# A recurrence's transposes moved from TensorE to VectorE and DMA, in three of seven groups

## The chip, the core and the metric

The kernel runs on one core of a Trainium2 chip. A core has TensorE (matrix products and transposes, called PE in the profile; its weight loads are shown apart as PEld), VectorE (DVE), ScalarE (ACT), GpSimd (POOL), and SyncE (SP), which here only issues DMAs. Each engine works through its own queue in order, and semaphores tie the queues together. The metric is the device time of one execution in microseconds.

## The reference

The input is x, 3327 tokens of 256 features in fp32, and a sparse adjacency matrix. Two layers follow. Layer 0 is graph attention with two heads, and then a mixture of 16 experts, of which each token takes two. Layer 1 is graph attention with one head, and then a recurrence. The change lies in the recurrence, which runs 30 steps on a state h of 3327 x 256:

```python
def step(h, _):
    h = h + 0.01 * jnp.tanh(h)
    h = h * jax.nn.sigmoid(h)
    h = _layernorm(h, ln_w, ln_b)
    h = jnp.einsum('bsc,dc->bsd', h, W) + b
    return (h, None)
```

The result of the recurrence is added to x. Tokens don't mix in the recurrence: a step is a chain for each token, and different tokens are independent.

## The kernel before, in words

Tokens lie on the 128 partitions: 26 tiles of 128 tokens, with the 256 features along the free dimension. The tile x in SBUF holds the state of all tokens; it stays on chip for all 30 steps. The recurrence (L865 to L902) loops over steps, and in a step over seven groups of tiles: six of four tiles, numbers 0 to 5, and number 6 of two.

For one group of a step:

- ScalarE takes the tanh (L871), GpSimd adds it to the state (L873), ScalarE applies silu (L874). The state is kept scaled by S = 100, so the factor 0.01 needs no instruction. The result is z.
- VectorE takes the statistics of z for each tile (bn_stats, L879, and bn_aggr, L859), and GpSimd makes 1/sqrt(var + eps) of them (L861, L862), called rr.
- The layer norm's mean, weight and bias are folded into the matrix beforehand: wc is the weighted matrix with its column mean taken out, and bb is the bias row (L833 to L846). So z can be multiplied without being normalized first, and rr is applied to the product.
- A product contracts over the features, and the operand that TensorE keeps as weights has to have them on the partitions. So TensorE transposes z, two blocks of 128 x 128 per tile, into the PSUM tile pt (L881), and ScalarE copies pt to SBUF as zT (L883).
- TensorE multiplies (L887): for each tile, two products with zT as weights and wc as the moving operand, added up in the PSUM tile po. [...]the trace has four matmul records a tile, 104 a step.
- VectorE writes the new state, x = po * rr + bb (L892).

In the last step the kept input is added (L899) and the output leaves by DMA.

Every tile of a group comes from a pool with a fixed number of buffers: th, z and zT have two each (pool "steps"), and so have the PSUM tiles pt and po[...]. A tile's next use waits until the readers of the buffer's earlier use are done.

The code is written in a straight line for one group after another. The framework that builds the program turns it into the engines' queues: it puts instructions that are ready by its own estimate in order of the program, and adds the semaphore waits. Thus the order on a queue is fixed before the run, and it is not the order of the source: in the trace, TensorE transposes two groups and then multiplies two groups. The names and lines above are those that the change touches; attend (L186, called at L829 for layer 1) is the attention that runs before.

Of the kernel before, what the change touches and what calls it, by code (L numbers as in the profile page):

```python
# [10 lines left out]
F32 = mybir.dt.float32  # L11
# [8 lines left out]
P = 128  # L20
# [3 lines left out]
S = 100.0  # L24
G = 4
MOST = 6


@with_exitstack
def gat_moe_gat_recurrent_ffn(ctx: ExitStack, tc: tile.TileContext, a: dict, out: bass.AP):  # L30
    nc = tc.nc
    N, D = a["x"].shape
    KD = D // P
# [9 lines left out]
    groups = [range(t, min(t + G, NT)) for t in range(0, NT, G)]  # L43
# [265 lines left out]
    lb = rec.tile([P, KD], F32, name="lb")  # L309
    fb = rec.tile([P, D], F32, name="fb")  # L310
    wc = rec.tile([P, KD, D], F32, name="wc")
    bb = rec.tile([P, D], F32, name="bb")
    ones_r = rec.tile([P, P], F32, name="ones_r")
    wv1 = rec.tile([P, KD, D + 2], F32, name="wv1")
# [453 lines left out]
    with ExitStack() as st:  # L768
        keep = st.enter_context(tc.tile_pool(name="keep2", bufs=1))
        wh = keep.tile([P, NT, 1, D + 1], F32, name="wh")  # L770
        sc = Scores(keep, 1)
        nc.vector.memset(wh[:, :, :, D : D + 1], 1.0)
        work = st.enter_context(tc.tile_pool(name="work2", bufs=2))
        ps = st.enter_context(tc.tile_pool(name="ps2", bufs=2, space=PSUM))
        ps_o = st.enter_context(tc.tile_pool(name="ps2o", bufs=2, space=PSUM))
        def add_results(some):
            for ts in some:
                n, two = len(ts), []
                for k, name in enumerate(("th", "z")):
                    here = slice(k * NP + ts[0] * P, k * NP + (ts[-1] + 1) * P)  # L780
                    two.append(steps.tile([P, G, D], F32, name=name)[:, :n, :])
                    nc.sync.dma_start(two[k], given[here, :].rearrange("(t p) d -> p t d", p=P))
                (nc.vector if ts is groups1[0] else nc.gpsimd).tensor_tensor(two[0], two[0], two[1], ALU.add)  # L783
                here = x[:, ts[0] : ts[-1] + 1, :]
                nc.vector.tensor_tensor(here, here, two[0], ALU.add)

        add_results(groups1[:2])
        count = 0

        def spot():  # L790
            nonlocal count
            count += 1
            return ps_o.tile([P, 512], F32, name=f"acc{count % 3}")

        def split1(t, p):
            nc.scalar.copy(wh[:, t, 0, :D], p[:, :D])
            nc.vector.tensor_copy(sc.s[:, t, :, 0], p[:, D : D + 2])
            for ts in groups1:
                if t == ts[-1]:
                    sc.finish(ts[0], t + 1)  # L800

        project(
            groups1, wv1, D + 2, split1, work, ps, spot, True,
            lambda ts, power: add_results(groups1[groups1.index(ts) + 2 :][:1]),
        )
        nc.vector.tensor_scalar(wh[:, NT - 1], wh[:, NT - 1], real[:, 0:1], None, op0=ALU.mult)

        run = st.enter_context(tc.tile_pool(name="edge2", bufs=3))
        rows_p = st.enter_context(tc.tile_pool(name="rows2", bufs=2))
        fin = st.enter_context(tc.tile_pool(name="fin2", bufs=2))  # L810

        def add_elu(t, pr, h, po, r):

            low = fin.tile([P, D], F32, name="low")
            high = fin.tile([P, D], F32, name="high")
            nc.vector.tensor_scalar(low[:pr], po, r, 0.0, op0=ALU.mult, op1=ALU.min)
            nc.vector.tensor_scalar(high[:pr], po, r, 0.0, op0=ALU.mult, op1=ALU.max)  # L817
            nc.scalar.activation(low[:pr], low[:pr], AF.Exp)
            nc.vector.scalar_tensor_tensor(high[:pr], low[:pr], -1.0, high[:pr], op0=ALU.add, op1=ALU.add)
            nc.vector.tensor_tensor(x[:pr, t, :], x[:pr, t, :], high[:pr], ALU.add)  # L820

        def begin_state(ts):
            here = slice(ts[0] * P, (ts[-1] + 1) * P)
            nc.sync.dma_start(kept[here, :].rearrange("(t p) d -> p t d", p=P), x[:, ts[0] : ts[-1] + 1, :])
            yield
            tiles = [x[:, t, :] for t in ts]
            normalized(tiles, tiles, S)

        attend(sc, wh, 1, groups2, 1, add_elu, begin_state, (run, rows_p, ps, ps_o), deque())  # L829

        pb = ps.tile([P, 512], F32, name="bank")[:, :D]  # L833
        for k in range(KD):
            nc.tensor.matmul(
                pb, lhsT=lb[:, k : k + 1].to_broadcast([P, P]), rhs=fW[:, k, :], start=(k == 0), stop=(k == KD - 1)
            )
        nc.vector.tensor_tensor(bb, pb, fb, ALU.add)
        nc.vector.tensor_scalar(bb, bb, S, None, op0=ALU.mult)
        pc = ps.tile([P, 512], F32, name="bank")[:, :D]  # L840
        for k in range(KD):
            nc.vector.tensor_scalar(wc[:, k, :], fW[:, k, :], lw[:, k : k + 1], None, op0=ALU.mult)
            nc.tensor.matmul(pc, lhsT=ones_r, rhs=wc[:, k, :], start=(k == 0), stop=(k == KD - 1))
        for k in range(KD):
            nc.vector.scalar_tensor_tensor(wc[:, k, :], pc, -1.0 / D, wc[:, k, :], op0=ALU.mult, op1=ALU.add)
            nc.vector.tensor_scalar(wc[:, k, :], wc[:, k, :], S, None, op0=ALU.mult)  # L846


    with ExitStack() as st:
        ps_t = st.enter_context(tc.tile_pool(name="ps3t", bufs=2, space=PSUM))  # L850
        ps_o = st.enter_context(tc.tile_pool(name="ps3o", bufs=2, space=PSUM))
        last_p = st.enter_context(tc.tile_pool(name="last", bufs=2))

        def inv_norm(stats, n):


            v = small.tile([P, G, 2], F32, name="v")
            for j in range(n):
                nc.vector.bn_aggr(v[:, j, :], stats[:, j, :])  # L859
            r = small.tile([P, G], F32, name="rr")  # L860
            nc.gpsimd.tensor_scalar(r[:, :n], v[:, :n, 1], EPS, None, op0=ALU.add)  # L861
            nc.gpsimd.tensor_tensor(r[:, :n], r[:, :n], neg_half[:, :n], ALU.pow)  # L862
            return r

        for step in range(N_STEPS):  # L865
            for ts in groups:
                n = len(ts)
                hs = x[:, ts[0] : ts[0] + n, :]
                th = steps.tile([P, G, D], F32, name="th")
                z = steps.tile([P, G, D], F32, name="z")  # L870
                nc.scalar.activation(th[:, :n, :], hs, AF.Tanh, scale=1.0 / S)  # L871

                nc.gpsimd.tensor_tensor(th[:, :n, :], th[:, :n, :], hs, ALU.add)  # L873
                nc.scalar.activation(z[:, :n, :], th[:, :n, :], AF.Silu, scale=1.0 / S)  # L874
                stats = small.tile([P, G, 6], F32, name="stats")
                pt = ps_t.tile([P, G, KD, P], F32, name="pt")
                zT = steps.tile([P, G, KD, P], F32, name="zT")
                for j in range(n):
                    nc.vector.bn_stats(stats[:, j, :], z[:, j, :])  # L879
                    for k in range(KD):  # L880
                        nc.tensor.transpose(pt[:, j, k, :], z[:, j, k * P : (k + 1) * P], ident)  # L881
                rr = inv_norm(stats, n)
                nc.scalar.copy(zT[:, :n, :, :], pt[:, :n, :, :])  # L883
                po = ps_o.tile([P, G, D], F32, name="po")
                for j in range(n):
                    for k in range(KD):
                        nc.tensor.matmul(  # L887
                            po[:, j, :], lhsT=zT[:, j, k, :], rhs=wc[:, k, :],
                            start=(k == 0), stop=(k == KD - 1),
                        )  # L890
                for j in range(n):
                    nc.vector.scalar_tensor_tensor(  # L892
                        x[:, ts[0] + j, :], po[:, j, :], rr[:, j : j + 1], bb, op0=ALU.mult, op1=ALU.add
                    )
                if step == N_STEPS - 1:
                    here = slice(ts[0] * P, (ts[-1] + 1) * P)
                    old = last_p.tile([P, G, D], F32, name="old")
                    nc.sync.dma_start(old[:, :n, :], kept[here, :].rearrange("(t p) d -> p t d", p=P))
                    nc.vector.scalar_tensor_tensor(  # L899
                        hs, hs, 1.0 / S, old[:, :n, :], op0=ALU.mult, op1=ALU.add  # L900
                    )
                    move_pairs(out, hs, ts[0] // 2, (ts[-1] + 1) // 2, True)  # L902
# [49 lines left out]
```

## Time and profile before

The kernel took 2091.18 us, the median of 3 runs (2089.25 to 2093.39). The profiled execution spans 2089.5 us at a mean granted TensorE clock of 0.979 of full speed.

| in the recurrence | per | number |
|---|---|---|
| TensorE products, L887 | 3120 records | 705.5 us busy |
| TensorE transposes, L881 | 1560 records | 189.9 us busy |
| GpSimd add, L873 | 210 instructions | 461.2 us busy |
| GpSimd power, L862 | 210 instructions | 207.5 us busy |
| VectorE state, L892 | 780 instructions | 324.9 us busy |
| VectorE statistics, L879 | 780 instructions | 283.8 us busy |
| ScalarE copy, L883 | 210 instructions | 199.1 us busy |
| ScalarE silu, L874, and tanh, L871 | 210 instructions each | 210.6 and 199.3 us busy |

How to read it: busy times of different engines lie beside each other, and do not add up. What sets the time is the engine that has no idle time, or a chain of instructions that wait for each other. A line of a timeline gives the start, the duration, engine, line, operation, the tile written and those read, and in square brackets how long the engine sat idle before and for whom. Names on the left of an arrow are written, those on the right are read. SPq is SP's queue of DMA issues; the duration there is that of the issue, not of the transfer.

### The profile page before, as it was taken

To read this page: it belongs to the slowest core of one execution; us is meant where nothing else is said; L and a number is where in the kernel's file an instruction comes from. 1 tells how busy PE (TensorE), PEld (TensorE's weight loads), DVE (VectorE), ACT (ScalarE), POOL (GpSimd) and SP (SyncE) were. 2 spreads that over 40 slices of the span, in tenths; PEclk is the share of its full clock that TensorE was granted. 3 is DMA by queue.
4 is the path that set the end of the run, shared out by engine and by line. 5 is a ranking of instruction groups with operands and counts; after the bars stand their busy time and mean duration, and the time that the engine had idled before them with its cause. 6 is when DMAs were issued, how large, how long until landed. Compare 5 with 4: busy or idle time off the path is not lost.

```text
span 2089.5 us, 34134 instructions
## 1 busy us (share of the span) xinstructions
PE 1974.8 (95%) x12252; PEld 1788.9 (86%) x12252; DVE 1304.8 (62%) x3824; ACT 1110.9 (53%) x1455; POOL 965.7 (46%) x896
## 2 busy tenths in 40 slices
PE   7999999749999997899999999999999999999998
PEld 6899999749999997688888888888888888888887
DVE  6787887712222222557766777777777777777777
ACT  2876766501111111656655666666566656665664
POOL 2010211343333332401100187777777777777775
PEclk9999999869999999899999999999999999999999
DMA  7878050067888883200000100000000000000003
GB/s 151 110 104 115 2 81 16 26 183 244 275 299 280 277 268 117 82 8 8 16 8 16 34 1 1 1 1 1 1 1 1 1 1 1 1 1 1 1 1 111
DMA packets 133438, 148.79 MB, mean 71 GB/s; under 512 B 51886, under 2 KB 95735, under 8 KB 133269
## 3 DMA queue, kind: packets, MB, share of 16 engines
q1 hardware_dynamic: 116577, 112.19, 17.9%
q0 software_dynamic: 12016, 29.66, 8.2%
q10 hardware_dynamic: 4676, 4.76, 0.8%
q8 instruction: 98, 1.61, 0.3%
q14 instruction: 71, 0.58, 0.1%
HBM read 174.37 MB, written 30.56 MB: 98 GB/s over the span
## 4 chain that ended last, share of the span: by engine, by line
PE 71%; ACT 5%; issue 1%; POOL 1%; DVE 1%; DMA 1%; SPq 0%; POOLq 0%; ACTq 0%; DVEq 0%
PE po L887 34%; PE acc L246 14%; PE pa L720 6%; PE pb L720 6%; PE po L751 6%; PE pt L881 4%; ACT zT L883 4%; PE pt L711 1%; PE acc L153 1%; POOL lists L551 0%; DMA z<-given 0%; PE bank L139 0%; POOL th L783 0%; DMA rows<-table_x,which 0%; POOL rstd L119 0%
## 5 line engine op out<-in xcount | busy, mean ns | idle before, releaser
L887 PE MATMUL po<-wc,zT 128*128 128x256 f32 x3120 | 705.5, 383 | 21.9 <-ACT zT L883 21.3
L887 PEld LDWEIGHTS po<-wc,zT 128*128 128x128 f32 x3120 | 582.9, 190 | 124.9 <-ACT zT L883 50.5
L246 PE MATMUL acc<-wh,pT 128*128 128x129 f32 (+1 forms) x4056 | 607.2, 311 | 7.0 <-DVE pT L241 6.7
L246 PEld LDWEIGHTS acc<-wh,pT 128*128 128x128 f32 x4056 | 563.7, 192 | 44.7 <-DVE pT L241 8.3
L236 ACT ACTIVATE e<-rb,minus,full 128x384 f32<-128x384 f32 (+3 forms) x494 | 401.3, 824 | 180.1 <-DVE pT L241 163.7
L873 POOL TENSOR_TENSOR th<-th,x 128x1024 f32<-128x1024 f32 (+1 forms) x210 | 461.2, 2214 | 63.7 <-ACT th L871 63.7
L241 DVE SCALAR_TENSOR_TENSOR pT<-e,part,adjT 128x384 f32<-128x384 f32 (+3 forms) x494 | 380.3, 773 | 146.3 <-PE acc L246 122.2
L892 DVE SCALAR_TENSOR_TENSOR x<-po,rr,bb 128x256 f32<-128x256 f32 x780 | 324.9, 477 | 118.2 <-PE po L887 113.4
L883 ACT COPY zT<-pt 128x1024 f32<-128x1024 f32 (+1 forms) x210 | 199.1, 948 | 332.7 <-PE pt L881 332.7
L879 DVE BATCH_NORM_STATS2 stats<-z 128x6 f32<-128x256 f32 x780 | 283.8, 415 | 117.5 <-ACT z L874 117.5
L119 POOL TENSOR_TENSOR rstd<-ve,neg_half 128x4 f32<-128x4 f32 (+3 forms) x28 | 31.2, 1116 | 408.0 <-DVE ve L117 312.4
L862 POOL TENSOR_TENSOR rr<-rr,neg_half 128x4 f32<-128x4 f32 (+1 forms) x210 | 207.5, 988 | 17.4
L874 ACT ACTIVATE z<-th 128x1024 f32<-128x1024 f32 (+1 forms) x210 | 210.6, 1003 | 0.9 <-POOL th L873 0.9
L871 ACT ACTIVATE th<-x 128x1024 f32<-128x1024 f32 (+1 forms) x210 | 199.3, 995 | 2.3 <-DVE x L128 1.4
L881 PE MATMUL pt<-ident,z 128*128 128x128 f32 x1560 | 189.9, 273 | 2.5 <-DVE high L817 2.5
L881 PEld LDWEIGHTS pt<-ident,z 128*128 128x128 f32 x1560 | 177.8, 141 | 14.8 <-issue 2.9
L744 DVE TENSOR_TENSOR hidT<-act,pb 128x512 f32<-128x512 f32 x67 | 46.1, 688 | 219.7 <-PE pb L720 216.2
L741 ACT ACTIVATE act<-pa 128x512 f32<-128x512 f32 x67 | 40.0, 597 | 205.1 <-PE pa L720 202.0
L720 PEld LDWEIGHTS pa<-hT,ew 128*128 128x128 f32 x1072 | 131.5, 194 | 5.0 <-ACT hT L712 1.7
L685 POOL DMA_INDIRECT rows<-table_x,which x67 | 64.6, 964 | 152.4 <-PE pt L711 136.8
L551 POOL DMA_INDIRECT lists<-pair,ati x52 | 60.2, 1157 | 160.8 <-DVE ati L538 85.2
L720 PE MATMUL pa<-hT,ew 128*128 128x128 f32 x1072 | 132.1, 277 | 1.0 <-ACT hT L712 1.0
(173 smaller groups left out, 1392.3 us busy)
## 6 DMA issues: line engine op xcount, KB each, us to landing
ew<-in_w_dram SPq DMA_DIRECT2D x201, 512.0 KB
in_bytes<-in_adj_dram POOLq DMA_DIRECT2D x3, 2496.0 KB, 28.2
x<-in_x_dram SPq DMA_DIRECT2D x6, 512.0 KB
th<-given SPq DMA_DIRECT2D x6, 512.0 KB
z<-given SPq DMA_DIRECT2D x6, 512.0 KB
kept<-x SPq DMA_DIRECT2D x8, 384.0 KB
old<-kept SPq DMA_DIRECT2D x6, 512.0 KB
out_dram<-x SPq DMA_DIRECT2D x6, 512.0 KB
```

Source lines behind the costliest of these rows:

```text
L236: nc.scalar.activation(e[:, : n * P], rb[:, : n * P], AF.Relu, scale=sc.full[:, j, h : h + 1], bias=sc.minus[:, j, h : h + 1],)
L241: masked = nc.vector.scalar_tensor_tensor(pT[:, : n * P], e[:, : n * P], sc.part[:, j, h : h + 1], adjT[:, j // 2, ts[0] * P : (ts[-1] + 1 ...
L246: nc.tensor.matmul(po[c], lhsT=pT[:, c * P : (c + 1) * P], rhs=wh[:, j, h, :], start=(j == 0 and c % per_bank == 0), stop=(j == NT - 1), s ...
L720: nc.tensor.matmul(p[:, f, :], lhsT=w[:, k, f * P : (f + 1) * P], rhs=hT[:, k, :], start=(k == 0), stop=(k == KD - 1),)
L862: nc.gpsimd.tensor_tensor(r[:, :n], r[:, :n], neg_half[:, :n], ALU.pow)
L873: nc.gpsimd.tensor_tensor(th[:, :n, :], th[:, :n, :], hs, ALU.add)
L874: nc.scalar.activation(z[:, :n, :], th[:, :n, :], AF.Silu, scale=1.0 / S)
L879: nc.vector.bn_stats(stats[:, j, :], z[:, j, :])
L881: nc.tensor.transpose(pt[:, j, k, :], z[:, j, k * P : (k + 1) * P], ident)
L883: nc.scalar.copy(zT[:, :n, :, :], pt[:, :n, :, :])
L887: nc.tensor.matmul(po[:, j, :], lhsT=zT[:, j, k, :], rhs=wc[:, k, :], start=(k == 0), stop=(k == KD - 1),)
L892: nc.vector.scalar_tensor_tensor(x[:, ts[0] + j, :], po[:, j, :], rr[:, j : j + 1], bb, op0=ALU.mult, op1=ALU.add)
```

## The change

Groups 0, 2 and 4 of every step no longer have z transposed by TensorE. VectorE transposes the blocks of 32 x 32 in one instruction over the whole group (128 x 1024), writing a tile tz in which the four tiles of the group are innermost. A block transpose turns each block, but leaves it in its own quarter of the partitions. So sixteen DMAs, from SBUF to SBUF, then move the quarters: quarter a of the partitions and feature blocks 2b and 2b + 1 of tz go to quarter b of a tile zx. Each moves 32 partitions times 1024 bytes, 32 KB, in runs of 512 bytes. All are issued by SP. The products read their weights from zx with a stride of four elements, 16 bytes. As the features now lie on the partitions in another order, the moving operand is wx, a copy of wc with its rows in that order, made once by eight small DMAs. The tiles tz and zx have two buffers each. For these groups the tiles pt and zT and ScalarE's copy fall away. Groups 1, 3, 5 and 6 stay as they were.

The purpose is to take work off TensorE. The call of the attention of layer 1 was moved behind the making of wc, bb and wx in the source, so that these come earlier in the program.

```diff
+QUAD = 32
...
+    wx = rec.tile([P, KD, D], F32, name="wx")
...
-        attend(sc, wh, 1, groups2, 1, add_elu, begin_state, (run, rows_p, ps, ps_o), deque())
-
...
+        for k in range(KD):
+            for q in range(4):
+                first = (2 * k + q // 2) * QUAD
+                nc.sync.dma_start(wx[first : first + QUAD, q % 2, :], wc[q * QUAD : (q + 1) * QUAD, k, :])
+
+        attend(sc, wh, 1, groups2, 1, add_elu, begin_state, (run, rows_p, ps, ps_o), deque())
...
+        swap_p = st.enter_context(tc.tile_pool(name="swap", bufs=2))
+
+        def exchanged(z):
+            tz = swap_p.tile([P, D // QUAD, QUAD, G], F32, name="tz")
+            nc.vector.transpose(
+                tz.rearrange("p b t j -> p j b t"), z.rearrange("p j (b t) -> p j b t", t=QUAD)
+            )
+            zx = swap_p.tile([P, KD, P, G], F32, name="zx")
+            for a in range(P // QUAD):
+                for b in range(P // QUAD):
+                    nc.sync.dma_start(
+                        zx[b * QUAD : (b + 1) * QUAD, :, a * QUAD : (a + 1) * QUAD],
+                        tz[a * QUAD : (a + 1) * QUAD, 2 * b : 2 * b + 2],
+                    )
+            return zx
...
-                pt = ps_t.tile([P, G, KD, P], F32, name="pt")
-                zT = steps.tile([P, G, KD, P], F32, name="zT")
+                swap = ts in groups[0:6:2]
+                if swap:
+                    zx = exchanged(z)
+                else:
+                    pt = ps_t.tile([P, G, KD, P], F32, name="pt")
+                    zT = steps.tile([P, G, KD, P], F32, name="zT")
                 for j in range(n):
                     nc.vector.bn_stats(stats[:, j, :], z[:, j, :])
-                    for k in range(KD):
-                        nc.tensor.transpose(pt[:, j, k, :], z[:, j, k * P : (k + 1) * P], ident)
+                    if not swap:
+                        for k in range(KD):
+                            nc.tensor.transpose(pt[:, j, k, :], z[:, j, k * P : (k + 1) * P], ident)
                 rr = inv_norm(stats, n)
-                nc.scalar.copy(zT[:, :n, :, :], pt[:, :n, :, :])
+                if not swap:
+                    nc.scalar.copy(zT[:, :n, :, :], pt[:, :n, :, :])
...
-                            po[:, j, :], lhsT=zT[:, j, k, :], rhs=wc[:, k, :],
-                            start=(k == 0), stop=(k == KD - 1),
+                            po[:, j, :], lhsT=zx[:, k, :, j] if swap else zT[:, j, k, :],
+                            rhs=(wx if swap else wc)[:, k, :], start=(k == 0), stop=(k == KD - 1),
```

## The prediction, made before the changed kernel was run

> **What bounds the kernel now.** I read the page's 40 slices first, then the busy time in a window of the recurrence, then the chain of work that ended last inside that window, then the timeline of one pair of groups, then the waits.
>
> The slices split the span. The recurrence is the last 17 or so of 40: TensorE at 9 tenths throughout, VectorE and GpSimd at 7, ScalarE at 6, DMA engines at 0.
>
> ```profile
> PE   7999999749999997899999999999999999999998
> DVE  6787887712222222557766777777777777777777
> ACT  2876766501111111656655666666566656665664
> POOL 2010211343333332401100187777777777777775
> DMA  7878050067888883200000100000000000000003
> ```
>
> Eleven steps of it, busy us for each engine:
>
> ```profile
> 1607.00:1937.00 330.00, 322.22 (x1721) 279.95 (x1722) 240.74 (x863) 209.04 (x233) 261.09 (x233) 1.00 0.00 1
> ```
>
> The block of 32 matmuls that starts at 1606.96 starts again at 1636.86, so one step takes 29.90 us, and 30 steps 897 us: they run from 1186 us, the first transpose, to the end. Per step TensorE is busy for 29.2 us (98%), VectorE 21.8, GpSimd 23.7, ScalarE 18.9. The clock is 1.00, so no throttle is to be won back.
>
> The chain in this window, in order of time:
>
> ```profile
> 1606.96 7.17 PE po L887 x32
> 1614.14 0.89 PE pt L881 x8
> 1615.03 0.02 issue
> 1615.05 1.02 ACT zT L883
> 1616.07 0.04 issue
> 1616.11 7.17 PE po L887 x32
> ```
>
> A pair of groups (8 tiles) is one turn of 9.15 us. The products take 7.17, the first group's transposes 0.89, then comes ScalarE's copy of 1.02, under which TensorE makes the second group's transposes. From the timeline of the same turn:
>
> ```profile
> 1606.81 1.06 ACT L874 ACTIVATE z<-th 128x1024 f32<-128x1024 f32 x1
> 1606.96 7.17 PE L887 MATMUL po<-wc,zT 128*128 128x256 f32 x32 [0.23 <-ACT zT L883]
> 1613.97 1.91 PE L881 MATMUL pt<-ident,z 128*128 128x128 f32 x16
> 1616.11 7.17 PE L887 MATMUL po<-wc,zT 128*128 128x256 f32 x32 [0.23 <-ACT zT L883]
> ```
>
> The square brackets give TensorE's only wait: 0.23 us a pair. And z of the next pair is ready at 1607.87, yet its products start at 1616.11: z leads them by **8.2 us**. VectorE's waits are slack, since what it waits for is TensorE or the z that TensorE's pace holds back:
>
> ```profile
> DVE stats L879 <- ACT z L874: 45.2, 78, 1.1
> DVE x L892 <- PE po L887: 42.2, 33, 1.5
> PE po L887 <- ACT zT L883: 7.8, 34, 0.2
> ```
>
> So TensorE sets the end, and its transposes (L881) lie on its path.
>
> [...]Both new strides (VectorE's write of tz, TensorE's weights from zx) are exactly 16 bytes, and nothing in this trace shows that case. [...]a 256 KB load issued at 826.45 released VectorE at 829.61, 3.2 us later, of which its bytes need about 1 at the 250 to 300 GB/s of the page's busy slices.
>
> **Removed.** For groups 0, 2 and 4 the eight transposes each: a half of the 1.91 us for sixteen, or the 0.89 of the chain. Three times 0.89 is **2.7 us a step on the path**, 80 us in 30 steps. Three ScalarE copies of 1.0 us go too, off the path, for ScalarE has 11 us idle a step. Three of seven uses of pt in PSUM go, and no wait in the window is put down to its buffers.
>
> **Added on VectorE.** One transpose of 128x1024 fp32 for each of three groups. [...]I take 1.25, with something for the waits on the buffer's earlier readers. VectorE goes from 21.8 to 25.6 us a step. That is within a TensorE-bound step (27.2), but at 94%, where its waits are no longer free. What is queued behind the transpose is the group's own bn_stats and the update of x (L892), for which the next tanh waits, with six other groups between: 1.25 us late there costs nothing alone.
>
> **Added on SP and the DMA engines.** Sixteen DMAs of 32 KB an exchange, each of 32 partitions. One issue is seen here:
>
> ```profile
> 826.03 0.38 SPq L782 DMA_DIRECT2D th<-given  x1
> 826.45 0.46 SPq L782 DMA_DIRECT2D z<-given  x1
> 826.97 0.46 SPq L782 DMA_DIRECT2D th<-given  x1
> 827.47 0.51 SPq L782 DMA_DIRECT2D z<-given  x1
> ```
>
> Starts lie 0.42 to 0.52 us apart. These are 512 KB or 256 KB; for 32 KB I take 0.42 (a one-row issue on L75 took 0.23, the lower end; 0.52 is the upper). Sixteen take 6.7 us (3.7 to 8.3), and the last lands some 2 us after its issue: an exchange is **8.7 us**, with the transpose ahead of it about 10. SP is then busy for 3 x 6.7 = 20 us of a step, 25 at most: not the bound, but close at the upper end. Bytes: 1.5 MB a step at 28 us is 55 GB/s, against 1 now and some 300 reached elsewhere; nothing.
>
> **Added waits on TensorE.** The products of a swapped group wait for all sixteen DMAs. Behind them in TensorE's queue are the next group's transposes and products, and behind these everything. The lead of z is 8.2 us today, the exchange needs about 10. But a swapped z gives its buffer back after VectorE's transpose and bn_stats (about 1.25 + 1.41 us), and not when TensorE comes to transpose it; so the z after next can be made earlier, until the two buffers of tz and zx are full. With two of each, exchange k+2 may start when the products of exchange k have ended, and between that and its own products lie two unswapped groups and one swapped one: 3 x 3.58 + 2 x 0.89 = 12.5 us. That covers 10. So I put the wait at nearly nothing, if the order on the queues allows it.
>
> **Weights with a stride.** A weight load takes 190 ns and lies beside the matmul before it, one per 224 ns (7.17/32). Unchanged if the stride is free; only above 224 would it count. I take nothing.
>
> **The early wc, bb and wx.** L835 to L846 ran at 1162 to 1172 us inside attention already; eight small DMAs more lie beside 100 us of attention. Nothing.
>
> **Sum.** TensorE's floor is 29.90 - 2.67 = 27.2 us a step. With VectorE at 94% and GpSimd at 87%, all in order with two buffers each, I add 0.7 us: 27.9. The gain is 30 x 2.0 = 60 us, so 2091 - 60 = **2031 us**.
>
> **Rivals.**
> 1. *The exchange is exposed.* If the order keeps today's distance of 8.2 us between z and its products, about 11 us of transpose, queueing and exchange leave some 3 us of wait: 3 x 3 x 30 = 270, less 80, or 2280 us: **slower**. For it: the order on an in-order queue was fixed beforehand, and no landing of such DMAs is in the trace. Against it: the buffer count above. A small exposure of 1 us each gives 2100.
> 2. *VectorE or SP becomes the bound.* Transposes of 2.2 us make VectorE 28.4 us busy; with a little waiting that is a 29.2 us step, 2070 us. SP at 0.52 an issue (25 us) acts likewise. For it: the unknown stride[...].
> 3. *Only TensorE counts*: 27.2 us a step, even less if the 0.23 us gaps close because a swapped group's products cover the copy: 26.6, 2091 - 99 = 1992 at best, 2010 likely.
>
> **Chances.** Forecast (2015 to 2055) 0.42; rival 3 (below 2015) 0.13; rival 2 (2055 to 2095) 0.18, of which 0.04 within 0.2% of before and 0.02 above; rival 1 0.27, of which 0.08 below 2160 (up to 1.7 us exposed each). Faster: 0.42 + 0.13 + 0.12 = 0.67; same 0.04; slower 0.29. The range leaves out the far part of rival 1, 0.19, and next to nothing below: 2000 to 2160.
>
> **What would show it.** Right: L881 with x840 of x1560 left; transposes on VectorE near 1.25 us; SP issues about 0.42 apart; steps near 27.9 us; TensorE still 95% in the recurrence's window; waits of TensorE on the DMA of zx small. Wrong: a large "PE po <- DMA zx" in the waits (rival 1), VectorE without idle time (rival 2), a weight load above 224 ns, or DMAs that land much later than 2 us because each waits for an earlier one (SP does wait for unrelated earlier DMAs at the start: L75 for lists<-zero, 4.9 us).

## The result and the profile after

The changed kernel took **2247.28 us**, the median of 4 runs (2242.66 to 2253.87), against 2090.22 us for the kernel before on the same chip: a ratio of 1.076, 95% interval 1.0719 to 1.0800. The forecast of 2031 us and its range (2000 to 2160) both miss: 2247 - 2031 = 216 us have to be found.

Attention ends at about 1183 us in both traces; the first transpose is TensorE's at 1186.20 before, and VectorE's at 1183.27 after. Thus moving the making of wx and the call of attention cost nothing that shows, and the whole difference lies in the 30 steps: (2244.7 - 1183) / 30 = 35.4 us each, against (2089.5 - 1183) / 30 = 30.2 before. This reckoning, used from here on, spreads the start and the end over the steps; the 29.90 us of the prediction is one step in the middle.

The slices of the kernel after:

```profile
PE   7999999399999979999997888888889888888886
...
PEclk9999999599999989999998899899998999999998
DMA  7975310468888831000002111111111111111114
```

TensorE has fallen from nines to eights, in a stage that was meant to keep it full with less work, and PEclk is no longer even either. The DMA engines are at 1 or 2 tenths for nearly all of it. The same eleven-step window as before (span, then busy us of PE, PEld, DVE, ACT and POOL, then the clock, DMA share and GB/s):

```profile
1607.00:1937.00 330.00, 285.36 (x1278) 251.41 (x1277) 260.25 (x788) 162.95 (x175) 230.16 (x203) 0.93 0.18 47
```

No engine in it is full. SP is missing from this view; its waits in the window (us in total, times, longest) are few:

```profile
SPq L873 <- DVE tz L867: 23.0, 15, 4.5
SPq L873 <- PE po L918: 2.3, 5, 0.6
...
```

SP waits for 25.7 of 330 us and issues for the rest, 465 DMAs: it is the fullest queue of the kernel. A stretch of the chain shows the pace of it: the issues are 0.59 us each with 0.04 between.

```profile
1699.72 0.59 SPq L873
1700.31 0.04 issue
1700.36 0.59 SPq L873
...
```

From start to start that is 0.64 us; sixteen take 10.2 us and the 48 of a step **30.5 us**. The groups of instructions that are new:

```profile
L918 PE MATMUL po<-wx,zx 128*128 128x256 f32 x1440 | 426.4, 459 | 132.3 <-DMA zx<-tz 50.1
L918 PEld LDWEIGHTS po<-wx,zx 128*128 128x128 f32 x1440 | 375.5, 329 | 181.0 <-DVE stats L908 66.4
...
L867 DVE STREAM_TRANSPOSE tz<-z 128x1024 f32<-128x1024 f32 x90 | 188.8, 2097 | 36.0 <-ACT z L899 25.9
L911 PE MATMUL pt<-ident,z 128*128 128x128 f32 x840 | 112.4, 279 | 25.6 <-ACT z L899 21.4
```

TensorE stood idle for 132.3 us ahead of the exchanged groups' products alone, and its mean product there is 459 ns where the others take 381; a weight load takes 329 ns, against 191 for the others. A part of these waits is put down to "DVE stats L908", but a product doesn't read those statistics. What the products at 1726.90 read is an exchange whose sixteen issues run from 1714.97 to 1725.15; with 1.75 us for the landing, which the chain shows for the exchange before it, that is 1726.90. The product waits for the sixteen DMAs. Their transpose had ended at 1708.14: the exchange stood 6.8 us in SP's queue before its first issue. VectorE's transpose takes 2.1 us and not 1.25. Three products from TensorE's timeline of the kernel after show what one block of sixteen can cost:

```profile
1705.27 5.60 PE L918 MATMUL po<-wx,zx 128*128 128x256 f32 x16 [1.88 <-DVE stats L908]
1716.71 4.08 PE L918 MATMUL po<-wx,zx 128*128 128x256 f32 x16 [0.33 <-DMA zx<-tz]
1726.90 6.77 PE L918 MATMUL po<-wx,zx 128*128 128x256 f32 x16 [2.67 <-DVE stats L908]
```

In these three the longer gap goes with the longer products. It isn't so throughout: the products at 1360.17 of this trace take 5.59 us after a gap of 3.71, and after one of 2.06 us at 1267.34 the clock stayed at 1.00. In the window from 1716.70 to 1720.80 the granted clock is 1.00, from 1726.90 to 1730.00 it is 0.50 and from 1730.00 to 1733.60 0.57. So a gap costs TensorE twice here: 2.67 us of waiting, and 6.77 - 4.08 = 2.7 us of slow products after it.

How much of each there is can be estimated from TensorE's time in the whole recurrence, before and after (columns as above):

```profile
1183.00:2089.50 906.50, 876.72 (x4684) 760.94 (x4682) 665.15 (x2348) 563.50 (x627) 700.72 (x623) 1.00 0.03 9
1183.00:2244.70 1061.70, 891.99 (x3960) 785.01 (x3960) 814.56 (x2436) 501.88 (x539) 700.46 (x623) 0.92 0.20 52
```

TensorE's idle time grew from 30 to 170 us. Its busy time grew by 15 us, although its transposes fell from 189.9 to 112.4 us, so 93 us came back in the products. By the blocks of sixteen at full clock, about 4.0 us in place of 3.62, the stride takes 34 us of these (90 blocks); the other 59 us or so go with a clock of 0.92.

### The profile page after: what moved, and what is told of

Read it like the earlier page. It is cut to its first block, busy times and chain, and to the rows that moved or that the text cites. A ratio compares the mean times of both kernels' runs of the same rounds, so it can differ in the third digit from the quotient of the medians.

```text
span 2244.7 us, 34913 instructions
## 1 busy us (share of the span) xinstructions
PE 1989.8 (89%) x11532; PEld 1810.8 (81%) x11532; DVE 1455.6 (65%) x3914; ACT 1048.8 (47%) x1367; POOL 964.3 (43%) x896
## 4 chain that ended last, share of the span: by engine, by line
PE 47%; SPq 14%; DVE 10%; issue 4%; DMA 3%; ACT 2%; POOL 1%; DVEq 0%; POOLq 0%; ACTq 0%
PE po L918 17%; SPq L873 14%; PE acc L247 12%; PE pa L722 5%; PE pb L722 5%; PE po L753 5%; DVE x L923 4%; DVE tz L867 2%; DMA zx<-tz 2%; DVE stats L908 2%; ACT zT L914 1%; ACT z L899 1%; PE pt L911 1%; PE pt L713 1%; PE acc L154 1%
## 5 line engine op out<-in xcount | busy, mean ns | idle before, releaser
L918 PE MATMUL po<-wx,zx 128*128 128x256 f32 x1440 | 426.4, 459 | 132.3 <-DMA zx<-tz 50.1
L918 PEld LDWEIGHTS po<-wx,zx 128*128 128x128 f32 x1440 | 375.5, 329 | 181.0 <-DVE stats L908 66.4
L923 DVE SCALAR_TENSOR_TENSOR x<-po,rr,bb 128x256 f32<-128x256 f32 x780 | 324.4, 485 | 195.1 <-PE po L918 187.3
L918 PE MATMUL po<-wc,zT 128*128 128x256 f32 x1680 | 381.5, 381 | 5.2 <-ACT zT L914 5.0
L918 PEld LDWEIGHTS po<-wc,zT 128*128 128x128 f32 x1680 | 318.2, 191 | 52.0 <-ACT zT L914 12.0
L908 DVE BATCH_NORM_STATS2 stats<-z 128x6 f32<-128x256 f32 x780 | 282.3, 421 | 14.1 <-ACT z L899 14.0
L896 ACT ACTIVATE th<-x 128x1024 f32<-128x1024 f32 (+1 forms) x210 | 204.9, 994 | 140.7 <-DVE x L923 86.6
L867 DVE STREAM_TRANSPOSE tz<-z 128x1024 f32<-128x1024 f32 x90 | 188.8, 2097 | 36.0 <-ACT z L899 25.9
L914 ACT COPY zT<-pt 128x1024 f32<-128x1024 f32 x120 | 106.9, 904 | 168.5 <-PE pt L911 163.0
L886 POOL TENSOR_SCALAR rr<-v 128x4 f32<-128x4 f32 (+1 forms) x210 | 48.2, 230 | 252.3 <-DVE v L884 182.3
L911 PE MATMUL pt<-ident,z 128*128 128x128 f32 x840 | 112.4, 279 | 25.6 <-ACT z L899 21.4
```

Of the source, the lines that this page charges most:

```text
L867: nc.vector.transpose(tz.rearrange("p b t j -> p j b t"), z.rearrange("p j (b t) -> p j b t", t=QUAD))
L918: nc.tensor.matmul(po[:, j, :], lhsT=zx[:, k, :, j] if swap else zT[:, j, k, :], rhs=(wx if swap else wc)[:, k, :], start=(k == 0), stop=( ...
L923: nc.vector.scalar_tensor_tensor(x[:, ts[0] + j, :], po[:, j, :], rr[:, j : j + 1], bb, op0=ALU.mult, op1=ALU.add)
```

## The experiments

Four theories are named in the expectations: A, the load of SP's issues sets the pace; B, VectorE's transposes do; C, the latency of the exchange is exposed; D, the products stand too early in TensorE's queue, so that they hold up work behind them that is ready. E and F come at the end, for what was then left. (One run uses the letter E for another theory, and says which.) Each ratio is to the kernel before, run beside the changed one, with its 95% interval.

**One DMA in place of sixteen.**

```diff
-            for a in range(P // QUAD):
-                for b in range(P // QUAD):
-                    nc.sync.dma_start(zx[b * QUAD : ...], tz[a * QUAD : ...])
+            nc.sync.dma_start(zx.rearrange("p k q j -> p (k q j)"), tz.rearrange("p b t j -> p (b t j)"))
```

> One DMA moves the whole of tz to zx, the same 512 KB an exchange, in place of sixteen; the partition quarters are not exchanged, so that part of the computation is left out. Theory A (SP's issues set the pace: 48 a step at 0.635 us each from start to start are 30.5 us of a 35.1 us step): SP falls to about 2 us a step, TensorE is no longer held up, its clock goes back to 1.00, and the step falls to what VectorE with 28 us busy allows, 28.5 to 30 us: 2045 to 2095 us. Theory B (VectorE with its transposes of 2.1 us and its in-order waits sets the pace): little changes, 2200 us or more. Theory C (the latency of an exchange of 10 us of issues and 2 of landing is exposed once per exchange, whatever SP's load): latency falls to 3 us, 2050 to 2100 us, like A.

Measured: 2125.98 us, ratio 1.0173 (1.0156 to 1.0190). Sixteen DMAs in place of one cost 121 us in this order, but a kernel with SP idle for 322.8 of 330 us is still slower than before, and slower than A or C had it. Theory A holds a part; C, which foretold much the same here, is not told apart from it. What is left shows already: in the window TensorE waits 30.5 us for ScalarE's copies, against 7.8 before.

**Two groups in place of three.**

```diff
-                swap = ts in groups[0:6:2]
+                swap = ts in groups[0:6:3]
```

> Only groups 0 and 3 are exchanged, with all sixteen DMAs each. Theory A: SP's load is 32 x 0.635 = 20.3 us a step, below the 28 us that TensorE needs, so the exchange of one group hides behind the other groups: 28.3 to 29.5 us a step, 2045 to 2080 us, faster than the kernel before. Theory B: VectorE has 26 us busy a step, 2040 to 2080 us. Theory C: each exchange still costs its exposed latency; the third of the loss goes with the third of the exchanges: 2190 to 2200 us.

Measured: 2298.68 us, ratio 1.0996 (1.0978 to 1.1014): with a third less of everything that the change added, 51 us *slower* than with three. SP now waits for 142.1 of the 330 us, so its load is not the bound, and A alone falls; B and C had less time as well. Five lines of this kernel's timeline show what is:

```profile
1702.30 21.79 SPq L873 DMA_DIRECT2D zx<-tz  x32
1706.45 1.91 ACT L914 COPY zT<-pt 128x1024 f32<-128x1024 f32 x2
1711.40 1.11 PE L911 MATMUL pt<-ident,z 128*128 128x128 f32 x4 [4.80 <-ACT z L899]
1714.23 5.57 PE L918 MATMUL po<-wx,zx 128*128 128x256 f32 x16 [1.72 <-DVE v L884]
1719.64 7.07 PE L918 MATMUL po<-wc,zT 128*128 128x256 f32 x32
```

The SP line folds two exchanges; the first one's sixteen issues end after 10.2 us, at about 1712.5. Its products start at 1714.23. The zT of two other groups is ready at 1708.36, yet their 32 products start at 1719.64: they stand behind the exchanged group's products in an in-order queue. In the 5.9 us from 1708.36 to 1714.23 TensorE made the four transposes at 1711.40 and sat idle for the other 4.8 us with that work ready, and the slow products after the gap come on top.

**ScalarE's copy in place of VectorE's transpose.**

```diff
-            nc.vector.transpose(
-                tz.rearrange("p b t j -> p j b t"), z.rearrange("p j (b t) -> p j b t", t=QUAD)
-            )
+            nc.scalar.copy(tz.rearrange("p b t j -> p (b t j)"), z.rearrange("p j d -> p (j d)"))
```

> A plain copy by ScalarE, 1.0 us, takes the place of VectorE's block transpose; the blocks are not transposed, so that part of the computation is left out. The sixteen DMAs stay. Theory A: SP is as loaded as before, 2200 to 2245 us. Theory B: VectorE falls from 28 to 22 us busy a step and the time to below 2100 us. Theory C: the latency falls by 1 us of 13: about 2200 us.

Measured: 2218.55 us, ratio 1.0612 (1.0594 to 1.0629). VectorE's busy time in the window falls from 260 to 211 of 330 us, and only 29 us come back, within what A gave. B is not what sets the pace of this kernel.

**Issues on two queues.**

```diff
-                    nc.sync.dma_start(
+                    (nc.sync if (a + b) % 2 == 0 else nc.scalar).dma_start(
```

> Every second DMA of an exchange is issued by ScalarE's queue, so SP has 24 issues a step (15 us) and ScalarE 24 (15 us, beside 16 us of work). Theory A: neither queue sets the pace, 2060 to 2130 us, more if ScalarE's tanh and silu wait behind its issues. Theory B: nothing changes, about 2240 us. Theory C: an exchange takes 5 us less, about 2120 us.

Measured: 2428.79 us, ratio 1.1621 (1.1602 to 1.1641). Halving the issues on a queue made it worse, as ScalarE's queue is not free: the reserve in A's forecast is what came. Its timeline:

```profile
1716.85 5.68 ACTq L873 DMA_DIRECT2D zx<-tz  x8
1722.57 1.01 ACT L914 COPY zT<-pt 128x1024 f32<-128x1024 f32 x1 [6.04 <-DMA zx<-tz]
```

Eight issues hold the queue for 5.7 us, and the copy that TensorE waits for stands behind them.

**The products placed later.** Theory D is tested by the order. The loop's body is cut in two: a front (tanh to statistics, transposes or exchange) and a back (products, new state). The back of an exchanged group is held until the back of a later group, and its products get an order edge behind that group's last product. The group's new state moves on VectorE's queue with its products:

```diff
+                if g in (0, 2, 4):
+                    held.append((step, *made))
+                    continue
+                last = back(step, *made, None)
+                for due in {1: (4,), 3: (0,), 5: (2,)}.get(g, ()):
+                    if held and held[0][1] == groups[due]:
+                        last = back(*held.popleft(), last)
```

> The changed kernel with one difference: on TensorE's queue the products of group 0 follow those of group 3, those of group 2 follow group 5, those of group 4 follow group 1 of the next step (an order edge, no wait). All sixteen DMAs and VectorE's transposes stay. Theory D (an exchange takes 12 to 14 us, but its products were placed in TensorE's queue as if it took some 4, and so they hold up ready transposes and products behind them): TensorE's waits on zx vanish and the step falls to what SP's 48 issues allow, 30.5 us, or a little more where single groups' copies are no longer covered: 2100 to 2150 us. Theory A (SP's issues already set the pace of the changed kernel, 35 us): no change, 2220 us or more.

Measured: 2305.95 us, ratio 1.1032 (1.1014 to 1.1051). D missed. The time lies where A had it, but the third run of this set, with one DMA, is as slow.

> Groups 0 and 3 exchanged, and the products of group 0 placed behind those of group 2, those of 3 behind group 5. Theory D: SP has 20.3 us of issues a step and no longer matters, the loss of the two-group kernel (2299 us) goes: 2055 to 2100 us. Theory A has no say here. If the time stays above 2200 us, the order is not what costs.

Measured: 2088.61 us, ratio 0.9997 (0.9987 to 1.0006). Against the same two groups in the old order (2298.68) the place of the products (and of the state that follows them) is worth **210 us**. In its window TensorE is back at 310 of 330 us busy and at full clock:

```profile
1607.00:1937.00 330.00, 310.48 (x1570) 279.75 (x1569) 277.83 (x900) 194.54 (x216) 266.44 (x237) 1.00 0.14 37
```

> One DMA of the whole tz in place of sixteen (the partition quarters are not exchanged, that part is left out) and the later place of the products. Theory D with A: nothing of the exchange is left on the path. What then remains over TensorE's 27.2 us a step is VectorE's 28 us and the uncovered copies: 28.5 to 31 us, 2045 to 2120 us. If VectorE's transposes are what is left, VectorE has no idle time.

Measured: 2298.34 us, ratio 1.0996 (1.0978 to 1.1014), as slow as the first of these three though SP has one DMA an exchange. So that one's fault is not the exchange but a place that is now too late: with one DMA and a nearer place for all three groups the time is 2113 us (below). Its waits in the window, with one DMA:

```profile
DVE tz L867 <- ACT z L893: 85.6, 27, 4.9
...
ACT th L890 <- DVE x L929: 47.2, 23, 4.2
```

Tanh waits for the new state: a state that is written late is missed at the start of the next step, and everything behind it moves. That group 4 is the one (its products came only in the next step) is a reading of these waits and was not tried by itself.

**The strides.** tz as [p, b, tile, t] and zx as [p, k, tile, q], so that neither VectorE's write nor TensorE's weights step over 16 bytes. The runs of the DMAs shrink to 128 bytes.

> The changed kernel with tz as blocks, tiles, columns and zx as halves, tiles, columns: VectorE writes and TensorE's weight loads read neighbouring elements, and each DMA moves the same 32 KB in runs of 128 bytes in place of 512. If the 16-byte step halves VectorE's rate, its transpose falls from 2.1 to 1.2 us[...]. The weight load falls from 329 to 190 ns, and 16 product records take 3.6 us in place of 3.9. The issue of a DMA stays at 0.6 us if it goes by the instruction, and grows if it goes by the runs. Theory D: with the same issues the time stays near 2200 us; with longer ones it grows by 3 x 30 x 16 x the difference at most.

Measured: 2494.55 us, ratio 1.1940 (1.1920 to 1.1960): far slower than the 2200 us expected, but each of the two operations shows its own price.

```profile
L918 PEld LDWEIGHTS po<-wx,zx 128*128 128x128 f32 x1440 | 332.0, 236 | 140.8 <-DVE x L923 63.9 <-issue 14.2 <-DVE stats L908 0.5
L867 DVE STREAM_TRANSPOSE tz<-z 128x1024 f32<-128x1024 f32 x90 | 112.0, 1245 | 9.6 <-DMA zx<-tz 1.2 <-ACT z L899 0.8 <-issue 0.6
```

The transpose takes 1.245 us and a weight load 236 ns in place of 329, in a kernel whose mean clock is 0.905 (at full clock, in the kernels below, 190). Why the whole got slower stays open. The issues don't explain it, for they hold SP for 0.61 us in place of 0.59. In the window TensorE waits 39.8 us for VectorE's new state (PE po <- DVE x L923), against 1.4 in the changed kernel, which points to another order on the queues; that was not tried by itself. In the later order below the same layout is a gain.

**Three groups, products behind the very next group** ({1: (0,), 3: (2,), 5: (4,)} in the loop above).

> The changed kernel, three groups and sixteen DMAs each, with the products of each exchanged group placed behind those of the next unswapped group of the same step (0 behind 1, 2 behind 3, 4 behind 5). Theory D (placed too early): the waits of ready work behind the exchange go, and SP's 48 issues become the bound, 30.5 us a step and some waiting: 2110 to 2170 us. Theory E (with three groups SP already sets the pace, so that the place of the products hardly matters): SP without idle time and 2200 us or more.

Measured: 2173.90 us, ratio 1.0410 (1.0382 to 1.0438). The order gives 73 us back, and the time is just above D's span. The sign that this run's E gave, SP without idle time, has come as well: SP waits in the window for 6.1 of 330 us, of which its waits for VectorE's transpose are

```profile
SPq L873 <- DVE tz L867: 4.4, 4, 1.3
...
```

The 324 us left hold 493 DMAs, 0.657 us each with some longer ones among them. At 48 a step that is 31.5 us, and a step in this window is 330 / 493 x 48 = 32.1 us: SP's issues bound this kernel.

**The same with one DMA** (the edit of the first experiment).

> As the first of this set with one DMA of the whole tz in place of sixteen (the quarters are not exchanged, that part is left out). Theory D: the products are now ready when their turn comes whatever the DMAs do; what is left is VectorE (28 us a step) and ScalarE's copies that nothing covers: 2060 to 2130 us. The difference to the first of this set is SP's share of the loss: 40 us or more if SP's issues bound it.

Measured: 2112.78 us, ratio 1.0107 (1.0082 to 1.0133): 61 us less for one issue and one landing in place of sixteen. With one DMA the place of the products is worth only 13 us (2126 to 2113), with sixteen 73: it counts for as much as the exchange is long. TensorE never waits for zx now, and its clock is 1.00, but it waits for ScalarE:

```profile
PE po L918 <- ACT zT L909: 35.7, 33, 1.5
```

Before, this wait was 7.8 us in the same window.

**Two groups with smaller strides**, both in the later order of 2089 us. First two half transposes, each over two tiles, so that the step is 8 bytes; then no step at all.

> The deferred two-group kernel (2089 us) with only two tiles innermost in tz and zx: a step of 8 bytes in place of 16 for VectorE's write and for the weights, DMA runs of 256 bytes. Its end was set by a chain through VectorE, so each us taken off the transpose comes back: with 8 bytes at full rate the two half transposes take 2 x 0.7 us in place of 2.1, 0.7 us twice a step, 42 us in all: about 2050 us. If 8 bytes cost what 16 do, no change or slightly slower, 2085 to 2100 us. If the exchange grows past its slack because of the shorter runs: slower than 2100 us.

Measured: 2070.97 us, ratio 0.9901 (0.9877 to 0.9926).

> The deferred two-group kernel with neighbouring elements in both places, and DMA runs of 128 bytes. VectorE's transpose falls from 2.1 to 1.25 us (measured with this layout): 0.85 us twice a step on the chain, 50 us: about 2040 us, if an exchange with runs of 128 bytes still fits behind the two groups it is hidden by (about 17 us between VectorE's transpose and the products there). If it doesn't, the products wait for zx and the time is above 2100 us.

Measured: 2068.54 us, ratio 0.9901 (0.9881 to 0.9922). A step of 8 bytes is as good as none within the intervals, and two groups are now 1% faster than the kernel before. But 18 and 20 us came back where 42 and 50 were expected: the chain through VectorE set only a part of the pace.

**Covering the copy.** After one DMA and the right side of the next group, 2113 - 2031 = 82 us were left. Theory E: ScalarE's copy of a lone unswapped group has nothing that covers it. Theory F: VectorE's slow transpose. The edit for E places the exchanged group's products between the next group's transposes and that group's products:

```diff
-                last = back(step, *made, None)
+                last = None
                 for due in {1: (0,), 3: (2,), 5: (4,)}.get(g, ()):
                     if held and held[0][1] == groups[due]:
-                        last = back(*held.popleft(), last)
+                        last = back(*held.popleft(), turned)
+                last = back(step, *made, last)
```

> As the kernel with one DMA for the exchange and each exchanged group's products placed behind the next group (2113 us, 31.0 us a step; it moves quarters nowhere, so zx is not the exchanged transpose here either), but the exchanged group's products are placed between the next group's transposes and that group's products, so that they cover ScalarE's copy, for which TensorE waited 35.7 us in eleven steps, 3.2 a step. Theory E (the gain that is still missing is the uncovered copy): three waits of about 1.1 us fall away, 28 us a step, 2020 to 2050. Theory F (VectorE's slow transpose, 2.1 in place of 1.25 us, sets that pace): the waits move elsewhere, 2090 to 2113. If zx comes too late for the earlier place: waits of TensorE on the DMA, over 2113.

Measured: 2039.90 us, ratio 0.9751 (0.9735 to 0.9768): 73 us back. Three blocks in a row in TensorE's timeline of this kernel, none with idle time ahead of it:

```profile
1707.66 1.04 PE L907 MATMUL pt<-ident,z 128*128 128x128 f32 x8
1708.54 4.00 PE L919 MATMUL po<-wx,zx 128*128 128x256 f32 x16
1712.37 3.62 PE L919 MATMUL po<-wc,zT 128*128 128x256 f32 x16
```

ScalarE's copy (1.01 us from 1708.74) lies wholly under the 4.00 us of the exchanged group's products. In the kernel of 2113 us, sixteen products after such a transpose had 1.45 and 1.10 us of idle time ahead of them.

> As the same kernel of 2113 us, but tz and zx without the 16-byte step, and the copy to zx in eight DMAs of 128 partitions (quarters are again moved nowhere, the data in zx is that of the 2113 us kernel). VectorE's transpose is 1.25 in place of 2.1 us, TensorE's weight load 190 in place of 329 ns. Theory E: only the 0.3 us a group of TensorE's strided products comes back, 30 x 3 x 0.3 = 27 us: 2080 to 2100. Theory F: VectorE's 0.85 us a group comes back as well, 30 x 3 x 0.85 = 76: 2010 to 2050. SyncE's 24 issues of 0.47 are 11 us a step and set nothing.

Measured: 2079.72 us, ratio 0.9942 (0.9925 to 0.9960), 33 us back: near the 27 us that E gave for TensorE's strides, and far from F's 76. TensorE still waits 33.8 us for the copies. (The issues took some 0.64 us each and not 0.47: seven of them lie between 1711.40, where a transpose ends, and 1716.17. At 24 a step, 0.68 from start to start, they are an estimated 16 us of a step of 29.8, so SP is not full.)

> Both of these edits together (quarters moved nowhere). Theory E: 1995 to 2025. Theory F: 2000 to 2040. Were both wrong and the chain through tanh, GpSimd's add, silu and the update of x set the pace: over 2060 whatever is done.

Measured: 2027.41 us, ratio 0.9682 (0.9663 to 0.9701), (2029.4 - 1183) / 30 = 28.2 us a step. It is 2 us over the span E gave and inside F's, so this run alone doesn't part the two. It is also 4 us below the forecast: the pace of the forecast exists, in a kernel that issues eight plain DMAs and exchanges nothing.

> The whole computation. As the two-group kernel without the 16-byte step (2069 us), but the exchanged group's products stand between the transposes and the products of the group that follows two later, so that they cover a copy. Theory E: the copies of the lone group cost it some 1 us twice a step, so 2020 to 2050. Theory F: VectorE has its fast transpose already; no change, 2060 to 2075. If the exchange of 12 us then lands too late: above 2069, with waits of TensorE on the DMA.

Measured: **2039.07 us**, ratio 0.9742 (0.9726 to 0.9759). The whole computation, and the fastest of all that do it: 51 us below the kernel before. Its exchanged products, placed this way:

```profile
1702.83 11.20 SPq L873 DMA_DIRECT2D zx<-tz  x16
1704.14 3.62 PE L924 MATMUL po<-wx,zx 128*128 128x256 f32 x16
1707.59 3.62 PE L924 MATMUL po<-wc,zT 128*128 128x256 f32 x16
```

The products at 1704.14 read the exchange before the one whose issues begin at 1702.83; that one's own start at 1717.18, 14.4 us later. It needs sixteen issues and a landing, 11.2 us by the line and 1.75 as in the kernel after, 13 us in all, and is hidden.

**The good order, with all sixteen DMAs and three groups.**

> The whole computation, three groups, all sixteen DMAs and the 16-byte step, in the order that gave 2040 us with one DMA (exchanged products between the next group's transposes and its products). If SyncE's issues are a bound by themselves, 48 of 0.635 us are 30.5 us a step, and no order goes below 1183 + 30 x 30.5 = 2098 us; with some waiting of TensorE and SyncE on each other 2100 to 2180. If they only delayed products that were placed wrongly, this order hides them too: 2040 to 2070.

Measured: 2244.13 us, ratio 1.0732 (1.0715 to 1.0750). Neither case: the place that is best with one DMA is too early with sixteen. SP waits for 31 of 330 us, and TensorE's waits on the exchange are back:

```profile
PE po L924 <- DVE stats L909: 19.1, 8, 3.5
PE po L924 <- DMA zx<-tz: 14.9, 10, 3.0
```

Hence how long an exchange is and where its products stand cannot be priced apart. This run also answers a doubt about the 73 us: it has the loop in two parts, as the kernel of 2174 us has, and differs from that in the order alone. So the gain is not one of the rewritten loop.

## Why the prediction was wrong, step by step

- **"The lead of z", and the wait put "at nearly nothing, if the order on the queues allows it".** This is the step that failed, and rival 1 the case that came. The lead of 8.2 us was that of the pair's first group; the second one's z was ready at 1609.73, 6.4 us ahead. I counted buffers: how early an exchange *may* start. What counts is where the products stand in TensorE's queue, and the order set beforehand put them ahead of work that was ready. The order alone is worth 73 us with three groups (2247 to 2174) and 210 us with two. The rival's 2280 us is near, but in part by luck: it was all waiting, 9 us a step. Lost were 2247 - (2091 - 80) = 236 us, 7.9 a step; TensorE's added idle time is 140 us of that, 4.7 a step, and the slow clock and the stride, some 93 us, were not in the rival's sum.
- **"SP ... not the bound, but close at the upper end".** This step failed too, and rival 2 came with it. I took 0.42 us an issue, with 0.52 as the upper end; it is 0.64 from start to start, so 20 us of SP a step became 30.5, above the forecast step of 27.9. The row I took it from showed loads of other shapes. In one order sixteen DMAs in place of one cost 61 us. In the best order found for sixteen DMAs and three groups (2174 us) SP is full, at 31.5 us a step with its longer issues. By itself, with nothing for the start and the end, that is an estimate of 1183 + 30 x 31.5 = 2128 us: enough to break the forecast without any error in the order.
- **"Three ScalarE copies ... off the path".** Rival 3 saw the gain, that a swapped group's products can cover a copy, but not the loss: the copies that *stay* came onto the path. Before, one group's copy lay under the next one's transposes; between two exchanged groups a lone one has no neighbour. 35.7 us in eleven steps are 3.2 a step, 97 us in thirty; the cover brought 73 us.
- **VectorE's transpose at 1.25 us.** This was my estimate, which nothing in the trace before showed. With the 16-byte step it takes 2.1, near the 2.2 of rival 2; without the step 1.245. It didn't set the pace: 29 us when taken away, and at most 12 to 33 us in the good orders, TensorE's strides included.
- **"Unchanged if the stride is free".** The stride isn't free: 329 ns against 190, above the 224 that I named as the limit, and sixteen products take 4.0 us in place of 3.62. That it is free was my assumption for both strides, and nothing in the trace before showed it. Measured, fp32 at four elements is dear on two engines (VectorE's transpose 2.1 us against 1.245, the weight load as above). At two elements it costs little here (two half transposes of 0.697 us against 1.245 for one; weights 196 ns). Why four elements cost so much more than two was not shown.
- **"No throttle is to be won back".** True of the kernel before. But with the waits the clock fell: 0.50 after a gap of 2.67 us, 0.92 over the recurrence, about 59 us by the estimate above. With one DMA in the same order it is 1.00 in the window. A lower clock was no term of the sum.
- **The removed part** was right: 840 records of L911 stay of 1560, and the kernel with one side of each cost taken away (2027 us) runs at 28.2 us a step by the reckoning that gives 30.2 for the kernel before: 2.0 less, as forecast. So was the landing "some 2 us after its issue": 1.75 us on the chain of the kernel after. Its issues made the exchange 12 us long, not 8.7.

From 2247 one path leads down to the forecast: order 73, issues 61, cover of the copy 73, strides 12, which is 2027. From the second term on the quarters are not exchanged. The terms are no independent sum, as the last experiment shows; in another sequence they would have other sizes. With 48 issues of 0.64 us on SP the floor is an estimated 1183 + 30 x 30.5 = 2098 us, so by this three groups can't go below the kernel before without fewer issues there; GpSimd's queue was not tried for a part of them. **Still open**: why the first deferred order costs as much as it does is argued from its waits only, and why the plain strides cost 247 us in the framework's order was not found.

## What to carry to other kernels

When work moves from an in-order engine to a slow detour, find the place in that engine's queue at which the result is consumed, and compare the landing time with that place: buffers say how early it may start, not how late it may come. Too early a place holds up ready work (210 us here), too late a place starves the next iteration (2298 against 2113 us here, with one DMA). Count DMA issues like instructions of an engine, with a price from the same shape (0.59 us each in the kernel after, where I had taken 0.42 from larger ones), and ask of each operation you leave in place which removed neighbour had covered it.

## What the runs showed of the hardware

- A DMA from SBUF to SBUF of 32 partitions and 32 KB holds SP for 0.59 us with runs of 512 bytes (the next starts 0.64 after it) and 0.61 with runs of 128. One of all 128 partitions holds it for 0.465 us with 512 KB in one piece a partition, and for some 0.64 with 64 KB in runs of 128 bytes, by the estimate above. In these the price does not go by the bytes moved.
- VectorE's block transpose of 128x1024 fp32 takes 1.245 us with the tiles apart, 2 x 0.697 with an 8-byte step and 2.1 with 16 bytes.
- TensorE's fp32 weight load takes 190 ns, 196 at 8 bytes and 329 at 16.
- TensorE's granted clock was 0.50 and then 0.57 for some 7 us after one idle gap of 2.67 us in an otherwise busy stretch, and 0.92 over that recurrence. The 33 gaps of up to 1.5 us in the window of the 2113 us kernel left it at 1.00.
- Eight DMA issues on ScalarE's queue held up its next copy for their whole length, 5.7 us.
